# The weights' preparation and the first eight tiles of an FFN, in one order written out pass by pass

## The chip, the cores and the metric

The kernel runs on one core of a Trainium2 chip. The metric is the time of one execution on the device in microseconds (us). The engines go by the profile's names: PE is TensorE, DVE VectorE, ACT ScalarE, POOL GpSimd; SP issues most DMAs.

## The reference

The input x is 2 x 2048 x 256 in fp32. A feed-forward half step, an attention and a second half step are added to it, each after a layer norm without weights:

```python
x = x + 0.5 * ffn(layernorm(x), w_gate, w_up, w_down)
x = x + attn(layernorm(x), Wq, bq, Wk, bk, Wv, bv, Wo, bo)
x = x + 0.5 * ffn(layernorm(x), w_gate, w_up, w_down)

def fp4_quant_dequant(x):          # blocks of 16 along the last dimension
    scale = max(abs(xb)) / 6, at least 1e-12
    return (nearest of 0, .5, 1, 1.5, 2, 3, 4, 6 to abs(xb / scale)) * sign * scale
def fp4_linear(x, w): return fp4_quant_dequant(x) @ fp4_quant_dequant(w).T
def ffn(x): return fp4_linear(silu(fp4_linear(x, w_gate)) * fp4_linear(x, w_up), w_down)
```

w_gate and w_up are 704 x 256, w_down is 256 x 704. The attention has one head of complex numbers: scores from the real and imaginary parts of 512 projected columns, a softmax over 2048 positions, and an output projection. Both half steps use the same three weights.

## The kernel before

The 4096 tokens are 32 tiles of 128 tokens, kept in SBUF as four groups of eight (xs[0] to xs[3]). A tile lies with its tokens on the 128 partitions and 256 columns. All arithmetic is fp32.

**Rounding** (quant). One call rounds y to the fp4 grid, in place, for several tiles at once: a maximum over blocks (DVE), the scale and its reciprocal (DVE, small), a multiplication by the reciprocal (DVE, or POOL for weights), abs(y) x 2^22 into m (ACT), two DVE passes that add and subtract a multiple of the step so that y is rounded, and a multiplication by the scale ("last": mostly POOL). It is used on the weights (1536 columns of gate and of up, 1408 of down), on the normed inputs xl of four tiles (1024 columns), and on the hidden values h of two tiles (1408 columns).

**Weights.** gate_or_up(0), gate_or_up(1) and down() round a weight and transpose it on PE in blocks of 128 x 128 into wgu and wd, with ACT copying PSUM to SBUF. fold() multiplies the attention's weights with each other (wa, wvo and three vectors): 12 transposes and then matmuls on PE, copies on ACT.

**A half step** (ffn, a generator; `stage` is the one under way). For four tiles at a time, inputs(i0) computes the layer norm (statistics on DVE, a square root on ACT, the rest on DVE, the normed values on ACT), rounds them and transposes them into xqT. products(i) makes gate and up of tile i on PE, each in one of two PSUM buffers (p_big), then silu(gate) on ACT and the product with up on DVE, which goes to h. After two tiles, h is rounded. turn(i) transposes a tile's h on PE (ACT copies it to hqT) and back(i) multiplies it by wd on PE; DVE adds half of the result to x. Tile i's turn and back come two to four tiles after its products.

**Order.** The source emits whole steps one after another: fold(), then the first inputs(0), gate_or_up(0), gate_or_up(1), the first products, down(), and so on; `next(stage)` between them advances the half step by one tile. From this, the Tile framework's scheduler makes an order for each engine: it takes ready instructions by priority (their place in the source), so that passes of several steps mix on an engine, and puts in the semaphores between engines. An engine then works through its own list in order. In the loads, gate and up come first on SP's queue, then wq, wk, wv, wo, down, the second half of the first x group, and at last the other three groups.

```python
    fold()
    stage = ffn(0, False, ffn0_pools)
    next(stage)
    gate_or_up(0)
    gate_or_up(1)
    next(stage)
    down()
    next(stage)
    prep.close()
```

The attention and the second half step follow in later code, overlapped with the end of the first half step; the change leaves them as they are.

Of the kernel before, what the change touches and what calls it, by code (L numbers as in the profile page):

```python
# [10 lines left out]
FP = mybir.dt.float32  # L11
# [16 lines left out]
BELOW = 1.0 - 2.0**-22  # L28


@with_exitstack
def kernel(ctx: ExitStack, tc: tile.TileContext, x, wqT, bq, wkT, bk, wvT, bv, woT, bo,
# [44 lines left out]
    for name, w in (("gate", w_gate), ("up", w_up)):  # L77
        t = wpool.tile([P, NR, D], FP, tag=f"n_{name}", name=f"n_{name}")
        nc.gpsimd.memset(t[LAST:P, NR - 1, :], 0.0)
        nc.sync.dma_start(  # L80
            out=t[:, 0:NR - 1, :], in_=w[0:(NR - 1) * P, :].rearrange("(r p) k -> p r k", p=P)
        )
        nc.sync.dma_start(out=t[0:LAST, NR - 1, :], in_=w[(NR - 1) * P:FF, :])
        w_nat.append(t)
# [4 lines left out]
    for t, w in ((wq_sb, wqT), (wk_sb, wkT), (wv_sb, wvT), (wo_sb, woT)):  # L89
        nc.sync.dma_start(out=t, in_=w.rearrange("(k p) e -> p k e", p=P))  # L90
    wd_nat = wpool.tile([P, KD, FF], FP, tag="n_down", name="n_down")
    nc.sync.dma_start(out=wd_nat, in_=w_down.rearrange("(r p) k -> p r k", p=P))
    nc.sync.dma_start(out=xs[0][:, 4:GT, :], in_=x_g[0][:, 4:GT, :])
# [19 lines left out]
    wd = const.tile([P, NR, D], FP, tag="wd", name="wd")  # L113
    wa = const.tile([P, KD, D], FP, tag="wa", name="wa")
# [39 lines left out]
    def normalise(pool, g, j0, n):  # L154


        mv = pool.tile([P, n, 2], FP, tag="mv", name=f"mv{g}_{j0}")
        for j in range(n):
            st = pool.tile([P, 6], FP, tag="bn", name=f"bn{g}_{j0 + j}")
            nc.vector.bn_stats(st, xs[g][:, j0 + j, :])  # L160
            nc.vector.bn_aggr(mv[:, j, :], st)
        var = pool.tile([P, n], FP, tag="var", name=f"var{g}_{j0}")
        nc.vector.tensor_scalar(var, mv[:, :, 1], EPS, None, ALU.add)
        sd = pool.tile([P, n], FP, tag="sd", name=f"sd{g}_{j0}")
        nc.scalar.activation(sd, var, AF.Sqrt)
        rstd = pool.tile([P, n], FP, tag="rstd", name=f"rstd{g}_{j0}")
        nc.vector.reciprocal(rstd, sd)

        nc.vector.tensor_tensor(sd, rstd, rstd, ALU.mult)
        nc.vector.tensor_tensor(sd, sd, var, ALU.mult)  # L170
        nc.vector.tensor_scalar(sd, sd, -0.5, 1.5, ALU.mult, ALU.add)
        nc.vector.tensor_tensor(rstd, rstd, sd, ALU.mult)
        shift = pool.tile([P, n], FP, tag="shift", name=f"shift{g}_{j0}")
        nc.vector.scalar_tensor_tensor(shift, mv[:, :, 0], -1.0, rstd, ALU.mult, ALU.mult)
        return j0, rstd, shift

    def normed(dst, g, j, stats):
        j0, rstd, shift = stats
        k = slice(j - j0, j - j0 + 1)
        nc.scalar.activation(dst, xs[g][:, j, :], AF.Identity, bias=shift[:, k], scale=rstd[:, k])  # L180


    n_bank = 0

    def bank(shape, name):
        nonlocal n_bank
        n_bank += 1
        pool, tag = ((p_t, "t"), (p_acc, "acc"))[n_bank % 2]
        return pool.tile(shape, FP, tag=tag, name=name)
# [6 lines left out]
    def gate_or_up(which):  # L196

        t = w_nat[which]
        all_of(quant(wpool, t.rearrange("p r k -> p (r k)"), NR * D, "qw", nc.gpsimd, nc.gpsimd))
        for kc in range(KD):  # L200
            for r0 in range(0, NR, 4):
                rs = range(r0, min(r0 + 4, NR))
                ps = bank([P, 4, P], f"wt{which}_{kc}_{r0}")
                for r in rs:
                    nc.tensor.transpose(ps[:, r - r0, :], t[:, r, ts(kc, P)], ident)
                n = min(FF - r0 * P, 4 * P)
                nc.scalar.copy(
                    wgu[:, kc, ds(which * FF + r0 * P, n)], ps.rearrange("p r k -> p (r k)")[:, 0:n]
                )

    def down():
        all_of(quant(wpool, wd_nat.rearrange("p r k -> p (r k)"), KD * FF, "qw", nc.gpsimd, nc.gpsimd))
        nc.gpsimd.memset(wd[0:P - LAST, NR - 1, :], 0.0)
        for ic in range(NR):
            ps = bank([P, KD, P], f"wtd{ic}")
            for r in range(KD):
                nc.tensor.transpose(ps[:, r, :], wd_nat[:, r, chunk(ic)], ident)
            p0 = 0 if ic < NR - 1 else P - LAST
            nc.scalar.copy(wd[p0:P, ic, :], ps.rearrange("p r k -> p (r k)")[p0:P, :])

    def fold():
# [4 lines left out]
        for name, t in (("q", wq_sb), ("k", wk_sb), ("v", wv_sb)):  # L226
            e_sb = wpool.tile([P, KE, D], FP, tag=f"e_{name}", name=f"e_{name}")
            for c0 in range(0, KE, 2):
                ps = bank([P, 4, P], f"we_{name}{c0}")
                for c in range(2):  # L230
                    for kc in range(KD):
                        nc.tensor.transpose(ps[:, c * KD + kc, :], t[:, kc, ts(c0 + c, P)], ident)
                nc.scalar.copy(
                    e_sb[:, c0:c0 + 2, :].rearrange("p c d -> p (c d)"), ps.rearrange("p r k -> p (r k)")
                )
            nat[name] = e_sb
        for dst, left, right in ((wa, nat["q"], nat["k"]), (wvo, nat["v"], wo_sb)):
            for kc in range(KD):
                ps = bank([P, D], f"wm{kc}")
                for c in range(KE):  # L240
                    nc.tensor.matmul(
                        out=ps, lhsT=left[:, c, ts(kc, P)], rhs=right[:, c, :], start=(c == 0), stop=(c == KE - 1)
                    )
                nc.scalar.copy(dst[:, kc, :], ps)
        for kc in range(KD):
            ps = bank([P, 1], f"wb{kc}")
            for c in range(KE):
                nc.tensor.matmul(
                    out=ps, lhsT=nat["k"][:, c, ts(kc, P)], rhs=bq_sb[:, c:c + 1], start=(c == 0), stop=(c == KE - 1)
                )  # L250
            nc.scalar.copy(wkbq[:, kc:kc + 1], ps)
        for dst, row, right in ((wqbk, bk_sb, nat["q"]), (bout, bv_sb, wo_sb)):
            ps = bank([P, D], "wr")
            for c in range(KE):
                nc.tensor.matmul(
                    out=ps,
                    lhsT=row[:, c:c + 1].to_broadcast([P, P]),
                    rhs=right[:, c, :],
                    start=(c == 0),
                    stop=(c == KE - 1),  # L260
                )
            nc.scalar.copy(dst, ps)
        nc.gpsimd.tensor_tensor(bout, bout, bo_sb, ALU.add)
        bb = wpool.tile([P, KE], FP, tag="bb", name="bb")
        nc.gpsimd.tensor_tensor(bb, bq_sb, bk_sb, ALU.mult)
        ps = bank([P, KE], "wbb")
        nc.tensor.matmul(out=ps, lhsT=ones, rhs=bb, start=True, stop=True)
        nc.vector.tensor_reduce(bqbk, ps, AX.X, ALU.add)


    def ffn(phase, store, pools):
# [4 lines left out]

        def inputs(i0):

            g, j0 = divmod(i0, GT)
            if i0 < GT:  # L280
                stats[g] = normalise(small, g, j0, XT)
            elif j0 == 0:
                stats[g] = normalise(small, g, 0, GT)
# [5 lines left out]
            yield from quant(xp, xl.rearrange("p u d -> p (u d)"), XT * D, "qx", nc.gpsimd if i0 else nc.vector)  # L289
            yield  # L290
            xqT = xp.tile([P, XT, KD, P], FP, tag="xqT", name=f"xqT{phase}_{i0}", bufs=2)
            for u in range(0, XT, 2):
                ps = p_t.tile([P, 4, P], FP, tag="t", name=f"tx{phase}_{i0}_{u}")
                for v in range(2):
                    for kc in range(KD):
                        nc.tensor.transpose(ps[:, v * KD + kc, :], xl[:, u + v, ts(kc, P)], ident)  # L296
                nc.scalar.copy(
                    xqT[:, u:u + 2, :, :].rearrange("p u k t -> p (u k t)"), ps.rearrange("p r t -> p (r t)")
                )
            xqTs[i0] = xqT  # L300

        def products(i, xqT, h):
            halves = []
            for which in range(2):
                ps = p_big.tile([P, 2, 512], FP, tag="big", name=f"gu{phase}_{i}_{which}")
                for b2 in range(2):
                    for kc in range(KD):
                        nc.tensor.matmul(  # L308
                            out=ps[:, b2, 0:HALF],
                            lhsT=xqT[:, kc, :],  # L310
                            rhs=wgu[:, kc, ts(which * 2 + b2, HALF)],
                            start=(kc == 0),
                            stop=(kc == KD - 1),
                        )
# [478 lines left out]
```

## Time and profile before

| | |
|---|---|
| time, median of 3 runs | 1086.97 us (1086.94 to 1086.97) |
| the profiled execution: its own time, its span | 1089.07 us, 1087.3 us |
| mean granted clock of TensorE | 0.991 |
| first matmul, first gu matmul | 12.5 us, 44.2 us |
| DMA share, GB/s from 20 to 25 us; from 30 us on | 1.01, 419; near 0 |

The page gives busy times over the span, and then the span in 40 slices of 27.2 us with a digit for the share in tenths. A line of a group reads: source line, engine, operation, output and inputs, shapes and count, then busy time and mean nanoseconds of one, then the engine's idle time ahead of it and what ended that. Tiles are named as in the source: gu is the PSUM of gate and up (L308), po that of back (L335), th that of turn (L327), tx that of the inputs' transposes (L296); n_gate, n_up and n_down are the weights in their natural layout. A matmul of the source in fp32 stands in the profile as two instructions, a transpose as one. Passes of a DVE pass's line: L132 maximum, L138 or L143 (POOL) first multiplication, L147 abs on ACT, L148 and L150 the rounding, L152 last multiplication. The timeline gives start, duration, engine, line and operation of each instruction; an instruction's duration there includes the time that it is held up after it began.

### The profile page before, as it was taken

The page shows a single profiled execution, that of the slowest core. Times are in us where ns is not written, and L with a number is a line of the kernel's source. Part 1 is how long each engine was busy: PE and PEld are TensorE (multiplying, and loading weights), DVE is VectorE, ACT ScalarE, POOL GpSimd, SP SyncE. Part 2 cuts the span into 40 slices and gives each one's busy share as a digit, 9 for nine tenths or more (in the row PEclk, how much of TensorE's full clock was granted, in tenths as well). Part 3 has the DMA queues.
Part 4 walks back from the last instruction along what each step waited for, and adds up shares of the span by engine and source line. Part 5 has one row for each costly group of instructions (what it writes and reads, how often), then busy time and mean ns, then how long its engine had stood idle before and what let it go on. Part 6 is the DMA issues. An engine that isn't in the chain of part 4 may idle for free.

```text
span 1087.3 us, 11292 instructions
## 1 busy us (share of the span) xinstructions
PE 1050.2 (97%) x4206; PEld 737.0 (68%) x4206; DVE 816.3 (75%) x1359; ACT 472.1 (43%) x734; POOL 236.0 (22%) x135
## 2 busy tenths in 40 slices
PE   4698999999999999999999999999999999999998
PEld 4566777777776566667666666766655677777776
DVE  5999988886663798566588977768776597777575
ACT  3455545454335564346444453344343253433222
POOL 2413121211002111111113211212372112122110
PEclk9889999999999999999999999999999999999999
DMA  9000000000000000000000000000000000000001
GB/s 316 1 1 1 1 0 1 1 1 1 1 1 1 0 1 1 1 0 1 0 1 1 1 0 1 1 1 1 0 1 1 10 11 19 20 10 20 20 10 39
DMA packets 7270, 13.50 MB, mean 12 GB/s; under 512 B 1328, under 2 KB 3632, under 8 KB 6832
## 3 DMA queue, kind: packets, MB, share of 16 engines
q1 hardware_dynamic: 6112, 12.13, 3.1%
q10 hardware_dynamic: 1104, 0.66, 0.3%
q8 instruction: 33, 0.54, 0.2%
q14 instruction: 21, 0.17, 0.1%
HBM read 8.59 MB, written 4.19 MB: 12 GB/s over the span
## 4 chain that ended last, share of the span: by engine, by line
PE 87%; DVE 9%; ACT 2%; DMA 1%; issue 1%; POOL 1%; DVEq 0%; ACTq 0%; POOLq 0%
PE gu L308 26%; PE ps L494 18%; PE po L335 15%; PE m L591 14%; PE th L327 4%; PE poa L642 3%; PE z L569 2%; PE pu L472 2%; PE tx L296 1%; DVE st L529 1%; PE txa L410 1%; ACT xn L180 1%; DVE bn L160 1%; DMA x<-in_x_dram 0%; DMA n_up<-in_w_up_dram 0%
## 5 line engine op out<-in xcount | busy, mean ns | idle before, releaser
L308 PE MATMUL gu<-wgu,xqT 128*128 128x352 f32 x1024 | 320.6, 463 | 2.8 <-ACT h L318 2.8
L308 PEld LDWEIGHTS gu<-wgu,xqT 128*128 128x128 f32 x1024 | 190.1, 192 | 97.0 <-issue 4.4
L494 PE MATMUL ps<-uT,xT 128*128 128x512 f32 x512 | 232.3, 593 | 0.9 <-DVE most L506 0.9
L335 PE MATMUL po<-wd,hqT 128*128 128x256 f32 x768 | 176.3, 379 | 0.0
L335 PEld LDWEIGHTS po<-wd,hqT 128*128 128x128 f32 x768 | 144.9, 190 | 28.8 <-ACT zT L605 0.6
L494 PEld LDWEIGHTS ps<-uT,xT 128*128 128x128 f32 x512 | 95.1, 190 | 93.7 <-issue 81.2
L152 POOL TENSOR_TENSOR h<-h,qh_s 128x1408 f32<-128x1408 f32 x30 | 78.7, 2622 | 326.1 <-DVE h L150 250.5
L506 DVE TENSOR_TENSOR most<-ps,most 128x512 f32<-128x512 f32 x112 | 77.0, 687 | 92.9 <-ACT st L501 92.3
L501 ACT COPY st<-ps 128x512 f32<-128x512 f32 x128 | 74.5, 583 | 127.9 <-PE ps L494 127.5
L328 ACT COPY hqT<-th 128x512 f32<-128x512 f32 (+1 forms) x128 | 55.4, 481 | 170.6 <-PE th L327 168.5
L591 PE MATMUL m<-tw,xn 128*128 128x256 f32 x448 | 124.6, 379 | 0.0
L558 POOL TENSOR_TENSOR sums<-tw,sums 128x512 f32<-128x512 f32 x42 | 57.9, 1378 | 230.1 <-DVE tw L554 198.9
L530 ACT ACTIVATE st<-st 128x1024 f32<-128x1024 f32 x64 | 67.4, 1057 | 77.3 <-DVE st L529 76.8
L591 PE MATMUL m<-st,xn 128*128 128x256 f32 x336 | 100.0, 379 | 0.0
L319 DVE TENSOR_TENSOR h<-h,gu 128x704 f32<-128x704 f32 x64 | 56.4, 882 | 56.8 <-PE gu L308 54.3
L591 PEld LDWEIGHTS m<-tw,xn 128*128 128x128 f32 x448 | 85.0, 190 | 12.5 <-DVE tw L550 0.6
L529 DVE TENSOR_TENSOR st<-st,top 128x1024 f32<-128x1024 f32 x64 | 83.2, 1311 | 0.8 <-ACT top L525 0.8
L591 PEld LDWEIGHTS m<-st,xn 128*128 128x128 f32 x336 | 63.2, 190 | 26.2 <-issue 19.1
L148 DVE SCALAR_TENSOR_TENSOR h<-qh_m,h 128x1408 f32<-128x1408 f32 (+1 forms) x34 | 53.5, 1574 | 34.3 <-ACT qh_m L147 34.1
L318 ACT ACTIVATE h<-gu 128x704 f32<-128x704 f32 x64 | 48.2, 753 | 50.9 <-PE gu L308 50.9
L147 ACT ACTIVATE qh_m<-h 128x1408 f32<-128x1408 f32 (+1 forms) x34 | 44.4, 1306 | 44.2 <-DVE h L138 40.7
L327 PE MATMUL th<-ident,h 128*128 128x128 f32 x384 | 52.8, 273 | 1.1 <-ACT hqT L328 1.1
(156 smaller groups left out, 1239.8 us busy)
## 6 DMA issues: line engine op xcount, KB each, us to landing
out_dram<-x SPq DMA_DIRECT2D x15, 256.0 KB, 2.1
x<-in_x_dram SPq DMA_DIRECT2D x3, 1024.0 KB, 13.1
n_down<-in_w_down_dram SPq DMA_DIRECT2D x1, 704.0 KB, 8.2
n_gate<-in_w_gate_dram SPq DMA_DIRECT2D x1, 640.0 KB, 6.8
n_up<-in_w_up_dram SPq DMA_DIRECT2D x1, 640.0 KB, 8.3
x<-in_x_dram ACTq DMA_DIRECT2D x1, 512.0 KB, 5.3
wq_sb<-in_wqT_dram SPq DMA_DIRECT2D x1, 512.0 KB, 4.8
wk_sb<-in_wkT_dram SPq DMA_DIRECT2D x1, 512.0 KB, 5.6
```

What stands on the lines that cost most here:

```text
L152: last.tensor_tensor(yb, yb, scale.unsqueeze(2).to_broadcast([P, nb, BLK]), ALU.mult)
L308: nc.tensor.matmul(out=ps[:, b2, 0:HALF], lhsT=xqT[:, kc, :], rhs=wgu[:, kc, ts(which * 2 + b2, HALF)], start=(kc == 0), stop=(kc == KD - 1),)
L319: nc.vector.tensor_tensor(h, h, up, ALU.mult)
L327: nc.tensor.transpose(ps[:, r - r0, :], hq[:, chunk(r)], ident)
L335: nc.tensor.matmul(out=po, lhsT=hqT[:, r, :], rhs=wd[:, r, :], start=(r == 0), stop=(r == NR - 1))
L494: scored = nc.tensor.matmul(out=ps, lhsT=gr.of.xT[s][:, c, v, :], rhs=gr.uT[:, c, :], start=(c == 0), stop=(c == KD - 1),)
L501: nc.scalar.copy(piece[:, v, :], ps)
L506: seen = nc.vector.tensor_tensor(gr.most, ps, gr.most, ALU.max)
L529: nc.vector.tensor_tensor(piece, piece, gr.top.unsqueeze(1).to_broadcast([P, 2, Q]), ALU.subtract)
L530: nc.scalar.activation(piece, piece, AF.Exp, scale=SCALE)
L558: add(gr.sums, t[:, 1:3, :], gr.first[:, 1:3, :] if s == 1 else gr.sums, ALU.add)
L591: i = nc.tensor.matmul(out=gr.m[k], lhsT=left, rhs=right, start=first, stop=last)
```

## The change

The weights' preparation and the first eight tiles become 36 generators ("threads"), each of which yields after a single pass: f (fold), g0, g1, u0, u1 (halves of gate and of up, 768 columns each), d0, d1 (halves of down, 704 columns), n0, n1, n2 (layer norm statistics of tiles 0-3, 4-7, 8-15), x0 to x5 (inputs of two tiles each, 512 columns, tiles 0 to 11), p0 to p7 (products of a tile), h0 to h3 (rounding of two tiles' h), t0 to t3 and b0 to b3 (turn and back of a tile). A string in the source, ORDER, names 264 steps; each takes the named thread's next pass. Each instruction of the opening gets a dependency without a semaphore on the one ahead of it in its engine's list (fence), so the scheduler keeps that order; close_fences() does the same between the opening's last instruction on each engine and everything emitted later.

Beside that:
- ON_POOL says for each thread whether the first and the last multiplication are on POOL. For h0 to h3 the first goes from DVE to POOL; for x0 and x1 both are on DVE, as they were for the first four tiles.
- A small step of the reciprocal on the POOL way is a tensor_scalar instead of a scalar_tensor_tensor with ones.
- The loads: gate in two parts with wq between and wk behind, then up, wv, wo, the second half of the first x group, down. One load more.
- The memset of wd is emitted at the start. The last sum of fold is an accumulation on ACT, not a reduction on DVE. The weights' PSUM tiles come from p_acc alone, not from p_t and p_acc in turn. h has four buffers in the first half step, not three.
- After the opening, the half step goes on from tile 8 with tiles 4 to 7 waiting for their turn.

```diff
+ORDER = """
+n0 n0 n0 g0 g0 g0 g0 n0 n0 g0 n0 g1 n0 g1 n0 f n0 g1 g0 n0 f g0 f n0 f g1 n0 g0 g1 x1 u1 x0 x1 u0 x0
+f g1 f u0 g0 u1 g1 f x0 x1 g1 u0 x0 f n1 u1 g1 f f n1 u0 x0 n1 x0 x1 f n1 n1 u1 x1 n1 d1 u0 u1 x1 u0
+n2 g1 n1 n2 n1 f u1 x0 d1 g1 n1 x0 x1 x0 n1 f u1 g0 x0 n1 x1 g0 p0 n1 x3 u1 u0 x2 p1 u1 n2 p0 d0 u1
+x3 x1 u0 u0 x3 d0 d1 n2 d0 d1 d1 u1 p1 n2 x2 n2 u0 n2 x3 u0 x2 d0 x3 x1 n2 x3 x2 n2 p0 x3 x2 n2 d1
+x2 d0 n2 p0 d0 n2 x3 n2 p1 p3 x2 p1 n2 x2 f n2 d0 h0 p3 d1 d0 h0 n2 p2 d1 p2 h0 x3 x4 x3 p3 x4 h0 x4
+p3 p2 x2 p2 x4 x5 x5 h1 d0 x2 x5 p6 p4 x4 h0 h0 p6 p5 h1 x4 h0 p4 d1 x4 h0 x4 h1 p5 p4 p5 h1 h0 h1
+x5 p4 d0 p5 p7 x4 h1 h2 d1 t0 p7 d1 x5 h1 x5 h2 t0 h1 p6 x5 p6 h2 h2 t1 p7 h1 h2 p7 h3 x4 d0 t1 x5
+h2 b0 h3 t2 h3 x5 h3 t2 h2 b1 b0 t3 x5 h2 t3 h3 b1 h3 h3 b2 h2 h3 b3 b2 b3 h3
+"""
+TURNED = 4
...
+    load_rows(w_nat[0], w_gate, 0, NH)
+    nc.sync.dma_start(out=wq_sb, in_=wqT.rearrange("(k p) e -> p k e", p=P))
+    load_rows(w_nat[0], w_gate, NH, NR)
+    nc.sync.dma_start(out=wk_sb, in_=wkT.rearrange("(k p) e -> p k e", p=P))
+    load_rows(w_nat[1], w_up, 0, NR)
+    nc.sync.dma_start(out=wv_sb, in_=wvT.rearrange("(k p) e -> p k e", p=P))
+    nc.sync.dma_start(out=wo_sb, in_=woT.rearrange("(k p) e -> p k e", p=P))
+    nc.sync.dma_start(out=xs[0][:, 4:GT, :], in_=x_g[0][:, 4:GT, :])
     nc.sync.dma_start(out=wd_nat, in_=w_down.rearrange("(r p) k -> p r k", p=P))
-    nc.sync.dma_start(out=xs[0][:, 4:GT, :], in_=x_g[0][:, 4:GT, :])
...
+    class Rounding:
...
+        def turns(self, y, n):
...
+            nc.vector.tensor_reduce(scale, yb, AX.X, ALU.max, apply_absolute_value=True)
+            yield
+            nc.vector.scalar_tensor_tensor(scale, scale, 1.0 / 6.0, tiny.to_broadcast([P, nb]), ALU.mult, ALU.max)
+            yield
+            rec = self.tile("r", nb, self.bufs)
+            nc.vector.reciprocal(rec, scale)
+            yield
+            if self.first:
+                nc.vector.tensor_scalar(rec, rec, BELOW, None, ALU.mult)
+                yield
+                nc.gpsimd.tensor_tensor(yb, yb, by_block(rec), ALU.mult)
+            else:
+                nc.vector.scalar_tensor_tensor(yb, yb, BELOW, by_block(rec), ALU.mult, ALU.mult)
+            yield
+            m = self.tile("m", n, self.bufs_m)
+            nc.scalar.activation(m, y, AF.Abs, scale=STEPS)
+            yield
+            nc.vector.scalar_tensor_tensor(y, m, LEAST, y, ALU.max, ALU.add)
+            yield
+            nc.vector.scalar_tensor_tensor(y, m, LEAST, y, ALU.max, ALU.subtract, reverse1=True)
+            yield
+            (nc.gpsimd if self.last else nc.vector).tensor_tensor(yb, yb, by_block(scale), ALU.mult)
+            yield
...
+        def products(i):
+            gate = product(0, i)
+            yield
+            h = hs[i].rearrange("p (c i) -> p c i", c=2)
             nc.scalar.activation(h, gate, AF.Silu)
+            yield
+            up = product(1, i)
+            yield
             nc.vector.tensor_tensor(h, h, up, ALU.mult)
+            yield
...
+        for name in ORDER.split():
+            next(threads[name])
...
+        fence(begun)
+        return 8, list(range(TURNED, 8)), norms["n2"]
...
-    fold()
     stage = ffn(0, False, ffn0_pools)
     next(stage)
-    gate_or_up(0)
-    gate_or_up(1)
-    next(stage)
-    down()
-    next(stage)
     prep.close()
...
+    close_fences()
```

## The prediction

> **What bounds the kernel now.** I read the page's slices first, then the windows, the groups of TensorE up to 150 us, the chain and the timeline. The page:
>
> ```profile
> PE 1050.2 (97%) x4206; PEld 737.0 (68%) x4206; DVE 816.3 (75%) x1359; ACT 472.1 (43%) x734; POOL 236.0 (22%) x135
> PE   4698999999999999999999999999999999999998
> DVE  5999988886663798566588977768776597777575
> POOL 2413121211002111111113211212372112122110
> PEclk9889999999999999999999999999999999999999
> ```
>
> TensorE is full from the fourth slice (82 us) on. Before that it is not, and there DVE is at 9. The windows (time, PE, PEld, DVE, ACT, POOL, clock, DMA, GB/s):
>
> ```profile
> 35.00:40.00 5.00, 1.08 (x5) 1.08 (x6) 5.00 (x7) 0.00 (x0) 2.12 (x1) 0.65 0.00 0
> 50.00:55.00 5.00, 1.48 (x5) 0.71 (x5) 5.00 (x9) 1.86 (x2) 2.59 (x1) 0.86 0.00 0
> 105.00:110.00 5.00, 2.88 (x13) 2.13 (x12) 5.00 (x7) 1.73 (x4) 1.93 (x1) 0.82 0.02 3
> ```
>
> DVE is never idle while TensorE starves, and the granted clock sags after each gap. How much TensorE loses I take from counts, since its busy time holds slow matmuls too. Dense prices are in the chain of waits:
>
> ```profile
> 114.83 2.59 PE po L335 x12
> 117.42 0.66 PE th L327 x6
> 118.08 4.74 PE gu L308 x16
> ```
>
> So 0.296 us for a gu matmul, 0.216 for one of 256 columns, 0.11 for a transpose of h or weights, 0.13 for one of x. The groups up to 150 us:
>
> ```profile
> L308 PE MATMUL gu<-wgu,xqT 128*128 128x352 f32 x208 | 67.7, 477 | 2.8 <-ACT h L318 2.8
> L335 PE MATMUL po<-wd,hqT 128*128 128x256 f32 x95 | 21.8, 379 | 0.0
> L296 PE MATMUL tx<-ident,xl 128*128 128x128 f32 x40 | 7.0, 332 | 8.0 <-DVE xl L152 4.5 <-POOL xl L152 3.5
> ```
>
> 208 x 0.296 + 95 x 0.216 + 40 x 0.13 + 48 transposes of h x 0.11 = 92.6, and fold() with the weights' transposes 19.1 at the same prices: 111.7 us of work in 150. **TensorE loses 38.3 us**, 34.6 of it by 86 us; from 150 us on it is dense, so what the change takes off the 38.3 comes off the end.
>
> Who holds DVE shows in the timeline:
>
> ```profile
> 28.90 1.22 DVE L148 SCALAR_TENSOR_TENSOR xl<-qx_m,xl 128x1024 f32<-128x1024 f32 x1
> 29.13 3.66 POOL L152 TENSOR_TENSOR n_gate<-n_gate,qw_s 128x1536 f32<-128x1536 f32 x1 [8.44 <-DVE n_gate L150]
> 30.04 4.37 DVE L148 SCALAR_TENSOR_TENSOR n_up<-qw_m,n_up 128x1536 f32<-128x1536 f32 x1
> 74.63 2.60 POOL L152 TENSOR_TENSOR h<-h,qh_s 128x1408 f32<-128x1408 f32 x1 [10.51 <-DVE h L150]
> 75.74 1.56 DVE L132 TENSOR_REDUCE qh_s<-h 128x88 f32<-128x1408 f32 x1
> ```
>
> The POOL pass that began under a DVE pass took 3.66 instead of 2.80, and the DVE pass issued next 4.37 instead of 1.75: it ended one pass length after POOL did. A POOL multiplication and a DVE pass with two SBUF inputs run one after the other; a maximum (75.74) runs beside POOL undisturbed. Of the nine large POOL passes up to 86 us (22.6 us at their own length), 7.4 us, a third, has DVE work of the undisturbed kind beside it: nearly all of the passes at 37.88 and 74.63, little of the rest.
>
> The Trainium skill (SBUF — State Buffer, "Who interferes with whom") says the same of this port pair, an exclusive lock, and so speaks against a part of this change: giving POOL the first multiplication of h frees DVE of no port time. The trace agrees (4.37); the sum below goes by the rows alone.
>
> **The change, part by part.** The opening (weights and eight tiles) keeps its arithmetic; its passes become smaller and their order is written out per engine, with everything later behind it. Prices for the new sizes n by lines through rows: a DVE pass 0.07 + 0.00104 n (1.14, 1.53, 1.67 us at 1024, 1408, 1536 in the chain of waits), a POOL pass 0.22 + 0.00168 n (1.93, 2.59, 2.80). A half of gate or up (768) costs 0.87 on DVE and 1.51 on POOL; a pair of x tiles (512) 0.60 and 1.08; half of down (704) 0.80 and 1.40; a pair of h 1.53 and 2.59; a small one 0.10 on DVE. Halving thus adds about 0.07 to 0.2 us a pass; it is in the sums.
>
> *DVE's queue up to the point that matters.* TensorE has two PSUM buffers for products, so gate of tile 6 ("p6") waits until DVE has multiplied tile 3 ("p3", fourth step). Ahead of that, counted in ORDER: 12 half-weight passes 10.4; 19 x passes 11.4; 6 of down 4.8; one maximum of h 1.5; three h*up at 0.87, 2.6; 16 bn_stats at 0.34, 5.4, with aggregates 1.9; reciprocals 4.0; 34 small ones 3.4. Sum 45.5. It begins when x lands, 6.1 (DVE's first row).
>
> *POOL meanwhile:* 8 x 1.51 + 3 x 1.40 + 2 x 1.08 + 0.85 for fold's sums = 19.3. Laying DVE's maxima, bn_stats, reciprocals and h*up (PSUM input: 0.88 us at 74.48 under POOL as elsewhere) beside these passes in the order given, all are covered but x2's last (1.1), d0's last (0.9), g0's last (1.0), u0's last (0.7) and scraps: 5.0 us of stall.
>
> *Waits of DVE for loads and ScalarE:* before, 0.3 + 1.15 + 4.07 and small ones, near 6, the 4.07 being for the normed x behind copies on ScalarE. The order puts a second thread wherever ScalarE is in the chain; between 0 and 6 I take 3.
>
> So p6 starts at 6.1 + 45.5 + 5.0 + 3 = 59.6. TensorE has then done fold 15.5, half-weights 2.6, four x transposes 2.1, eight half products 19.0: 39.2. **Lost 20.4.** The first product starts near 30 (44.2 before), the first "up" near 39.
>
> *After p6:* 34.3 us of TensorE work (eight half products 19.0, down 1.3, x 1.1, turns and backs of four tiles 2.6 + 10.4), dense to 94, then tile 8's products to 98.7, then the turn of tile 4, which needs h2's last POOL pass. DVE up to h3's add, which runs ahead of that pass: 45.5 + 27.2 (seven x passes 4.2, ten h passes 15.3, five h*up 4.4, the rest 3.3) = 72.7. POOL ahead of it 38.4, of which 10.5 uncovered (h3's first 2.2, h2's first 1.1, h0's last 0.9 are the new ones of size). 6.1 + 72.7 + 10.5 + 2.6 + 3 = 94.9, before 98.7: no new stall.
>
> *Moved work.* h's first multiplication to POOL: 4 x 1.53 off DVE, 4 x 2.59 on POOL, both inside these sums; alone it is worth between -6.1 and +4.2. fold(), scattered over TensorE's gaps, costs nothing while those gaps exist (15.5 of work before p6, 20.4 lost); were they gone it would cost its length, as now. Its last reduction goes from DVE (0.15) to ScalarE, which was busy 37.9 of the 80 us from 6 to 86. The memset of wd goes to POOL's start: 0.3 hidden in its wait for the first maximum. Loads: wq second in SP's queue instead of fifth lands ahead of 12.5, where TensorE now begins; up lands some 2.5 us later (two 0.5 MB loads ahead at 400 GB/s, the windows' rate at 15 us), near 13.8, as DVE reaches it; x's second half goes ahead of down, both used past 19. One more load costs SP 0.5 us of issuing, ahead of all later loads, hidden likewise.
>
> *The pins.* Whatever waits holds all behind it on its engine: ScalarE's first copy of fold waits for wq with the absolute value of the first gate half behind it, and DVE's add behind that; this is in the 3 us. The end of the opening pins tile 8 and the inputs of tile 12 behind it; those are needed only at some 127, and DVE has 32 us for some 27 of work (one x of 1024, two h, four h*up, norms at the prices above).
>
> Remaining loss: 20.4, 1 for a sagging clock where TensorE waits for "up", 1 for stalls past p6 (3.7 past 86 before). 22.4 against 38.3 leaves a gain of 15.9.
>
> On the clock: the Trainium skill (TensorE: Matmul & The Clock Gate, Part 1) has half rate after an idle window of about 3.4 us until one busy window is over. The trace agrees in kind (0.65 in 35 to 40); by that rule a gap costs up to 1.7 us, and the sum with two more would be 3.4 us worse.
>
> The profiled execution took 1089.07 with a span of 1087.3; the median is 1086.97. The sum is made on the span's loss and its difference carried to the median: **1071 us**.
>
> **Rivals.** All turn on how much of POOL's time is covered, and on the waits.
> - *Covered as little as now, a third.* Ahead of h2's last pass: 6.1 + 72.7 + 25.7 + 2.6 + 3 = 110.1 against 78.3 of TensorE work: 31.8 lost, with 2 as above 33.8, a gain of 4.5: 1082.5. For it: no engine's order is tied to another's, so a shift of 1 us puts a POOL pass over another DVE pass than intended. Against: long runs of maxima and statistics stand where POOL runs.
> - *Slower: POOL locks DVE throughout.* The end rises with each uncovered us. With nothing covered, 38.4 in place of 25.7: 44.5 + 2 lost, 8 us slower: 1095. It decides where cover falls under 22%. For it: at 15.10 and 44.15 tiny DVE steps took 2.77 and 2.29 us under POOL, the new order has 24 large POOL passes up to h3 where the old one has 12, and a pinned DVE cannot go round a locked step. Against: the third reached now.
> - *Better.* Cover of 85% and 1 us of waits: 6.1 + 45.5 + 2.9 + 1 - 39.2 = 16.3, with 0.5 more 16.8, a gain of 21.5: 1065.5.
>
> **Numbers.** A measurement here can tell 0.2% (2.2 us) from no change. Forecast, 1066.5 to 1077: 0.55. Little cover, 1077 to 1084.8: 0.22. Better: 0.10. Slower: 0.10. Between, within 0.2%: 0.03. The likeliest is 1071; the range 1064 to 1084 leaves out about 0.05 below and 0.14 above. Faster 0.87, same 0.03, slower 0.10.
>
> **What would show it.** Right: first gu matmul near 30 and not 44, a dense TensorE from about 60, h2's last POOL pass ending near 95, the 150 us mark reached with some 16 us more TensorE work done, no change of the rest. Wrong: DVE passes of two inputs at 2.5 to 4 us in a row, h2's last pass past 105, TensorE gaps behind the opening, or another time in the rest of the kernel, whose order the scheduler chooses.

## The result, and the profile after

After: 1074.16 us, the median of 4 runs (1073.74 to 1074.85); before, beside it, 1086.97 (1086.94 to 1087.64, 4 runs). The ratio is 0.9881, 95% interval 0.9864 to 0.9898: 12.8 us faster, 3.2 us above the forecast of 1071. The profiled execution of after took 1073.74, with a span of 1071.9 and a mean granted clock of 1.000.

The page, busy times and the first lines of the slices (now 26.8 us each):

```profile
PE 1044.7 (97%) x4206; PEld 731.6 (68%) x4206; DVE 805.8 (75%) x1387; ACT 469.9 (44%) x739; POOL 253.6 (24%) x148
PE   6998999999999999999999999999999999999998
DVE  7999998867634888576688958678767587777575
POOL 4563121210103020111124111212461021221110
```

TensorE is at 9 from the second slice on, but for the fourth and the last, which are at 8 as they were before. POOL is busier in the first slices, and DVE has 10.5 us less of busy time over the span. The windows (time, PE, PEld, DVE, ACT, POOL, clock, DMA, GB/s), the three of before and one where a gap now lies:

```profile
35.00:40.00 5.00, 4.72 (x26) 3.29 (x26) 5.00 (x23) 3.74 (x9) 4.30 (x3) 1.00 0.00 0
50.00:55.00 5.00, 5.00 (x21) 3.34 (x20) 4.60 (x10) 3.25 (x7) 4.86 (x3) 1.00 0.00 0
95.00:100.00 5.00, 2.96 (x11) 1.57 (x9) 5.00 (x8) 1.70 (x2) 0.00 (x0) 1.00 0.01 2
105.00:110.00 5.00, 5.00 (x26) 3.96 (x25) 4.27 (x13) 4.49 (x7) 0.00 (x0) 1.00 0.00 0
```

In 50 to 55 all engines work at once. In 95 to 100 TensorE stands while DVE is full, as it did before in the opening. The groups of TensorE up to 150 us:

```profile
L428 PE MATMUL gu<-wgu,xqT 128*128 128x352 f32 x240 | 74.6, 461 | 2.4 <-DVE h L446 2.0 <-ACT xqT L404 0.3
L472 PE MATMUL po<-wd,hqT 128*128 128x256 f32 x120 | 27.5, 380 | 0.0
L403 PE MATMUL tx<-ident,xl 128*128 128x128 f32 x40 | 5.8, 275 | 3.9 <-POOL xl L184 3.9
...
L330 PE MATMUL we_q<-ident,wq_sb 128*128 128x128 f32 x8 | 1.9, 420 | 8.1 <-DMA wq_sb<-in_wqT_dram 8.1
```

240 gu matmuls stand where 208 did, and 120 of po where 95 did. At the prediction's dense prices 128.5 us of work are done by 150: TensorE loses 21.5 where it lost 38.3. The loss over time, so counted, in us:

| up to | 50 | 70 | 88 | 110 | 150 | 250 |
|---|---|---|---|---|---|---|
| before | 26.5 | 33.5 | 34.4 | 37.5 | 38.3 | 38.1 |
| after | 15.0 | 14.7 | 15.1 | 19.5 | 21.5 | 22.4 |

The last column counts the attention's first transposes too (txa, 0.13 each). So the opening gained 19.3 by 88, and 3.6 of it are given back between 88 and 250; the 15.7 that are left are near the 15.3 by which the two profiled executions differ. TensorE in the timeline:

```profile
30.88 5.00 PE L428 MATMUL gu<-wgu,xqT 128*128 128x352 f32 x16 [0.35 <-ACT xqT L404]
38.08 7.60 PE L428 MATMUL gu<-wgu,xqT 128*128 128x352 f32 x24
...
97.73 2.63 PE L428 MATMUL gu<-wgu,xqT 128*128 128x352 f32 x8 [2.04 <-DVE h L446]
102.41 1.09 PE L403 MATMUL tx<-ident,xl 128*128 128x128 f32 x8 [2.04 <-POOL xl L184]
125.81 1.09 PE L403 MATMUL tx<-ident,xl 128*128 128x128 f32 x8 [1.85 <-POOL xl L184]
```

From 31 to 88 us TensorE loses 1 us in all; the gaps at 97.7, 102.4 and 125.8 are the ones behind the opening. The locks between DVE and POOL:

```profile
21.34 0.68 DVE L277 SCALAR_TENSOR_TENSOR xl<-xl,qx_r 128x512 f32<-128x512 f32 x1
21.50 1.87 POOL L275 TENSOR_TENSOR n_up<-n_up,qw_r 128x768 f32<-128x768 f32 x1
62.48 1.86 DVE L273 TENSOR_SCALAR qh_r<-qh_r 128x88 f32<-128x88 f32 x1
79.96 3.90 POOL L275 TENSOR_TENSOR h<-h,qh_r 128x1408 f32<-128x1408 f32 x1
81.67 3.67 DVE L285 SCALAR_TENSOR_TENSOR h<-qh_m,h 128x1408 f32<-128x1408 f32 x1
```

L275 is the first multiplication on POOL, L277 the one on DVE, L273 the small step ahead of it, L285 the second rounding pass. At 21.50 POOL began second and paid (1.87, 1.49 alone); at 62.48 and 81.67 DVE paid: 1.86 (the pass of POOL there lasts from 61.38 to 64.28), where the same step took 0.19 with no POOL pass beside it at 80.22 in the kernel without closing pins below; and 3.67 in place of 1.62, behind POOL's pass of 79.96. That pass had itself paid before (3.90 in place of 2.59), as DVE's pass of 79.81 was under way. I took each pass's time above the usual one of its shape (excesses over 0.05 us) up to 88.1: DVE was held 7.5 us and POOL 6.2, with 47.9 us of POOL's passes. Before it was 10.5 and 1.7, with 26.4.

### The profile page after: what moved, and what is told of

It is laid out like the page before. It is cut to its first block, busy times and chain, and to the rows that moved or that the text cites. A ratio compares the mean times of both kernels' runs of the same rounds, so it can differ in the third digit from the quotient of the medians.

```text
span 1071.9 us, 11329 instructions
## 1 busy us (share of the span) xinstructions
PE 1044.7 (97%) x4206; PEld 731.6 (68%) x4206; DVE 805.8 (75%) x1387; ACT 469.9 (44%) x739; POOL 253.6 (24%) x148
## 4 chain that ended last, share of the span: by engine, by line
PE 89%; DVE 7%; ACT 2%; DMA 1%; issue 1%; POOL 0%; SPq 0%; DVEq 0%; ACTq 0%; POOLq 0%
PE gu L428 26%; PE ps L708 19%; PE m L805 15%; PE po L472 14%; PE th L463 4%; PE poa L856 3%; PE pu L686 2%; PE z L783 2%; PE tx L403 1%; DVE st L743 1%; PE wm L338 1%; PE txa L624 1%; ACT xn L234 1%; DVE h L285 1%; DVE h L283 1%
## 5 line engine op out<-in xcount | busy, mean ns | idle before, releaser
L184 POOL TENSOR_TENSOR h<-h,qh_s 128x1408 f32<-128x1408 f32 x26 | 67.5, 2595 | 294.0 <-DVE h L182 252.1
L180 DVE SCALAR_TENSOR_TENSOR h<-qh_m,h 128x1408 f32<-128x1408 f32 (+1 forms) x30 | 45.8, 1527 | 33.1 <-ACT qh_m L179 32.9
L442 ACT ACTIVATE h<-gu 128x704 f32<-128x704 f32 x64 | 48.2, 753 | 44.9 <-PE gu L428 44.6
L179 ACT ACTIVATE qh_m<-h 128x1408 f32<-128x1408 f32 (+1 forms) x30 | 38.9, 1297 | 45.9 <-DVE h L170 42.1
```

Source lines behind the costliest of these rows:

```text
L184: last.tensor_tensor(yb, yb, scale.unsqueeze(2).to_broadcast([P, nb, BLK]), ALU.mult)
```

## The experiments

Times are medians, and the loss is TensorE's, counted as above. The main theory: the gain is the order, pinned on each engine, by which POOL's passes lie beside DVE passes that they don't hold. The rivals: the parts alone make it (smaller passes, the loads, h's multiplication on POOL), or DVE's sum of work decides and not the locks.

The kernel before was timed anew with each group of runs, with medians from 1086.96 to 1087.85. For the three changes of 2.2 to 3.0 us below, the interval of the ratio overlaps with that of after; that they are slower rests on their times, all of which are above the slowest of after (1074.85), and on the loss counted by 150 us (24.3 to 25.6, after 21.5).

**Without the pins.** The same passes, emitted in the same order; the scheduler sets each engine's list.

```diff
-        fence(begun)
...
-    close_fences()
```

> The changed kernel without its fences: the same single passes emitted in the same order, but the scheduler is free to reorder on each engine. Theory A (the gain is the order itself, DVE and POOL passes laid beside each other): the scheduler departs from it, DVE is locked more often by POOL; 1077 to 1085, over 3 us slower than the changed kernel's 1074.2. Theory B (the gain comes from smaller passes and from emitting the threads together; the pins do nothing): 1073 to 1076.

1085.76 (1083.52 to 1086.48, 11 runs; the profiled one, 1083.62, is among the fastest); ratio to before 0.9978 (0.9969 to 0.9987). Of the 12.8 us all but 1.4 need the pins: smaller passes, loads and POOL's multiplications without them are worth next to nothing. The loss by 88 us is 25.4 (after 15.1). Locks are only a part of these 10.3: DVE was held 11.1 us, 3.6 more than in after, with less work of POOL (39.2 us). Other parts stand in TensorE's waits, of which ScalarE's list has two:

```profile
PE we_k L330 <- ACT e_q L331: 3.7, 1, 3.7
PE po L472 <- ACT wd L313: 3.3, 1, 3.3
```

The columns are the sum, the number and the longest, up to 150 us. The first was 1.4 in after; the second, from 85.4 to 88.6, isn't there in after. The first gu comes at 34.55. How the 10.3 divide between locks and the rest isn't shown. So the theory holds for the order as a whole and is too narrow in naming the locks alone.

**Pinned, but thread after thread.** The other bound of the same theory: the 264 steps in the order f, n0, x0, x1, g0, g1, u0, u1 and so on, each thread to its end.

> The changed kernel with its 264 steps in another order, as pinned: each thread runs to its end before the next begins (fold, n0, x0, x1, g0, g1, u0, u1, n1, x2, x3, p0, p1, h0 and so on). Theory A (the gain is the weave; pins without it keep every engine waiting for the one step under way): the opening's DVE 75 us, POOL's 43 and ScalarE's share of the chains add up with little beside each other, TensorE loses 60 to 90 us in place of 15: 1105 to 1145. Rival (fixed lists of smaller passes do it in any sensible order): 1074 to 1087.

1202.4 (ratio 1.1051, 1.1036 to 1.1067), slower than even the theory gave. One window (columns as above), and the longest of TensorE's waits up to 150 us:

```profile
50.00:75.00 25.00, 4.63 (x18) 3.42 (x18) 15.59 (x24) 6.13 (x10) 10.43 (x8) 0.50 0.00 0
PE wtd L311 <- POOL n_down L287: 25.4, 2, 20.5
```

No engine is full: each waits for another in turn. The loss is 110.2 us by 150, and 143.8 by 250: tile 8 onwards has been held behind it all. Of the 110.2, TensorE stands still for 95.7, so the waits alone exceed the theory's 60 to 90. Another 14.9 are matmuls slower than the dense prices; the theory's price had left out the clock, 0.50 in this window. Pins alone don't gain; the weave that they hold does.

**Without the closing pins only.** Order pinned inside the opening; later work may be placed among it.

```diff
-    close_fences()
```

> The orders stay pinned inside the opening, but the work written behind it is free to be placed among it by the scheduler (the closing fences are left out). Theory: the pinned order of the opening is what gains, and the closing fences only keep later work behind it, so 1072 to 1078 with the first gu product still near 31 us and TensorE's loss up to 50 us near 15 us. Rival: work of tiles 8 to 12 placed among the opening takes VectorE's and POOL's time from the chain to h, loss up to 88 us of 18 us or more, 1078 to 1086.

1076.71 (ratio 0.99, 0.9883 to 0.9916): 2.5 slower than after. First gu at 30.53 and loss by 50 us of 15.6, as the theory had it, but by 88 us 20.8, as its rival had it:

```profile
78.09 2.20 DVE L180 SCALAR_TENSOR_TENSOR xl<-qx_m,xl 128x1024 f32<-128x1024 f32 x1
81.13 3.03 DVE L182 SCALAR_TENSOR_TENSOR xl<-qx_m,xl 128x1024 f32<-128x1024 f32 x1
...
88.03 1.11 PE L403 MATMUL tx<-ident,xl 128*128 128x128 f32 x4 [2.37 <-POOL xl L287]
```

L180 and L182 round tile 12's inputs, work due over 20 us later, and they are held (2.20 and 3.03, some 1.2 alone); the last multiplication of the opening's own inputs then comes 8 us later on POOL (86.92, after 78.77), and TensorE waits for it. Part of the loss comes back by 150, since those inputs are done: 24.7 against 21.5.

**h's first multiplication back on DVE.** The weave is the same, without the four small steps.

```diff
-    ... "h0": (True, True), "h1": (True, True), "h2": (True, True), "h3": (True, True),
+    ... "h0": (False, True), "h1": (False, True), "h2": (False, True), "h3": (False, True),
```

> The changed kernel with the first multiplication of h0 to h3 back on DVE (four steps fewer in the order). By the port (a POOL pass and a two-input DVE pass run one after the other) 4 x 2.59 us of POOL go and 4 x 1.53 us of DVE come: between 4 us faster and 1 us slower, as the opening's end or only its cover counts: 1070 to 1075. By DVE's busy time alone, which is what the step in the change would be for: 3 to 6 us slower, 1077 to 1080.

1080.55 (ratio 0.9932, 0.9919 to 0.9944): 6.4 slower than after, a miss of the port theory, and 0.5 beyond what DVE's busy time alone gave. DVE was held 4.8 us by 88, 2.7 less than in after, but it has 6.1 us more of its own work, and what remains is still locked:

```profile
65.36 3.28 DVE L277 SCALAR_TENSOR_TENSOR h<-h,qh_r 128x1408 f32<-128x1408 f32 x1
67.13 2.43 POOL L287 TENSOR_TENSOR xl<-xl,qx_s 128x512 f32<-128x512 f32 x1
```

The loss is 19.0 by 88 and 30.1 by 150. So the four POOL passes, 10.4 us long, cost DVE 2.7 us and freed it of 6.1; the rest lay mostly beside maxima, reciprocals and h*up.

**h's first multiplication of tiles 8 to 15 on POOL too**, where no order is written out.

```diff
-            all_of(quant(later["pool"], h, n * FF, "qh", nc.gpsimd if n == HT else nc.vector))
+            ahead = nc.gpsimd if first and i0 < 16 else None
+            all_of(quant(later["pool"], h, n * FF, "qh", nc.gpsimd if n == HT else nc.vector, ahead))
```

> The changed kernel, where the four pairs of tiles behind the opening (tiles 8 to 15) too have h's first multiplication on POOL. Theory A (TensorE's 6.4 us lost between 88 and 150 us are DVE's backlog; taking four passes of 1.54 us off DVE takes most of it away, as the same four passes cost 6.4 us in the opening): 3 to 5 us faster, 1069 to 1071. Rival (there POOL's 4 x 2.59 us lock DVE out of its two-input passes): 0 to 4 us slower, 1074 to 1078.

1080.54 (ratio 0.9931, 0.9919 to 0.9944): 6.4 slower than after, the way of the rival and beyond its 0 to 4. The move that gains 6.4 in the weave loses 6.4 outside it. One reason stands at 108.07, 0.2 us behind the start of a POOL pass (107.89 to 110.48):

```profile
108.07 2.43 DVE L221 TENSOR_TENSOR rstd<-rstd,sd 128x8 f32<-128x8 f32 x1
```

A step on 8 numbers a partition, 0.15 us alone, waits for that pass to end; another, at 153.05, takes 2.35. The move isn't quite the same, either: the small step ahead of the multiplication is a scalar_tensor_tensor with two SBUF inputs here, which took 1.71 at 128.67 and 1.56 at 151.15 under POOL's passes (0.23 elsewhere). Loss up to 250 us: 29.3, after 22.4.

**The small step ahead of POOL's multiplication moved to POOL**, at its old place in the order.

```diff
-                nc.vector.tensor_scalar(rec, rec, BELOW, None, ALU.mult)
+                nc.gpsimd.tensor_scalar(rec, rec, BELOW, None, ALU.mult)
```

> The changed kernel with the small step in front of POOL's first multiplications (a tensor_scalar on 44 to 88 columns) on POOL in place of DVE. On DVE, this step took 1.86 and 1.07 us at 62.5 and 74.3 where POOL was in a pass, and 0.2 us elsewhere. Theory A (a tensor_scalar in SBUF is locked out by POOL as a two-input pass is): the step leaves DVE's queue, some 3 us of DVE time go, POOL gains ten small steps of 0.2 to 0.3 us in its idle time: 1 to 3 us faster, 1071 to 1073. Rival (the step merely shows a wait that the next DVE pass would take in its place): no change, 1073.5 to 1075.

1079.84 (ratio 0.9927, 0.9914 to 0.9941): 5.7 slower, a miss. The step was put into POOL's list where DVE's had stood:

```profile
53.00 0.43 POOL L273 TENSOR_SCALAR qh_r<-qh_r 128x88 f32<-128x88 f32 x1 [6.37 <-DVE qh_r L270]
53.40 1.06 POOL L287 TENSOR_TENSOR xl<-xl,qx_s 128x512 f32<-128x512 f32 x1
```

POOL stood 6.37 us for DVE's reciprocal, with the last multiplication of x2 behind it: 53.40, after 45.97. A pinned list turns one misplaced step of 0.4 us into a stall of everything behind it.

**The same, with the step directly ahead of its multiplication in the order.**

> The small step on POOL once more, but with its place in the order moved right in front of the multiplication that it serves, so that it holds nothing else in POOL's list. The earlier run, 1079.8, had it ahead of x2's last multiplication, which started at 53.4 in place of 46.0, behind the small step's wait for a reciprocal of h0. Theory A (that place alone made it slower, and the tensor_scalar on DVE was locked out by POOL for some 3 us): 1 to 3 us faster than the changed kernel, 1071 to 1073. Rival (POOL's small step is itself on the path, 0.3 to 0.4 us in each of ten chains, or DVE's gain moves to another wait): 1073.5 to 1077.

1076.32 (ratio 0.9893, 0.988 to 0.9907): the wait is gone, and it is still 2.2 slower. DVE was held only 4.4 us by 88, but the step lengthens each chain to h: 0.32 to 0.98 us on POOL, up to 1.80 when DVE holds it, for 0.2 to 0.36 on DVE where POOL did not hold it for long. That this is the reason isn't shown: by 88 us only 0.9 more is lost than in after (16.0), and the rest comes behind the opening (24.3 by 150).

**The loads in the old order** (gate and up, then wq, wk, wv, wo, down, x's second half).

> The changed kernel with the loads in the order of the kernel before (gate, up, wq, wk, wv, wo, down, x's second half). Theory A (a pinned list waits for its slowest item): ScalarE's copy of fold's first transposes waits for wq near 12.5 in place of 8.1, and behind it stands the absolute value of gate's first half, 11.3 in the changed kernel; DVE's first add goes from 12.4 to some 15.5, and 2 to 4 us reach the end: 1076 to 1078. Rival (DVE has other work to put there and TensorE's start doesn't count): 1073.5 to 1075.

1077.15 (ratio 0.9898, 0.9883 to 0.9913): 3.0 slower. The first transposes begin 4.5 us later (12.66, after 8.11), and, through the copy on ScalarE that is pinned ahead of the absolute value of gate, DVE's first rounding pass at 15.15 (12.35). Loss by 50 us: 17.9, after 15.0.

**Behind the opening: tile 12's inputs emitted two tiles later.**

```diff
-            if i0 % XT == 0 and i0 + XT < NT and i0 + XT not in xqTs:
+            if i0 % XT == 0 and i0 + XT < NT and i0 + XT not in xqTs and i0 != first:
                 all_of(inputs(i0 + XT))
+            if first and i0 == first + HT:
+                all_of(inputs(first + XT))
```

> The changed kernel with the inputs of tile 12 emitted two tiles later, behind the products of tiles 8 and 9 in place of ahead of them. In the changed kernel TensorE stands still for 2.0 us before 97.7 and 2.0 us before 102.4, where DVE does these inputs before it multiplies h of tile 8. Theory A (the stalls come from that place in the source alone): both gaps vanish and nothing takes their place, 4 us faster, 1069.5 to 1071. Rival (DVE is behind by then whatever it does first, so the wait only moves to tile 12 or 16): 1073 to 1076.

1073.96 (ratio 0.9874, 0.986 to 0.9887), no change, as the rival said. The wait at 102.4 went, and one of 3.84 for the same kind of input came at 128. DVE's list hardly changed up to 101 us: tile 8's h*up, now earlier in the source, still began at 96.80 behind tile 12's first passes (96.81 in after). That isn't because it wasn't ready: pinned ahead, in the last run below, it began at 93.77.

**Only the transposes later.** Inputs stay where they are but for the transposes and their copies, which are emitted ahead of the products of the group's last tile. The edit reaches all five groups behind the opening, not only the two that the expectation names.

```diff
-            if i0 % XT == 0 and i0 + XT < NT and i0 + XT not in xqTs:
-                all_of(inputs(i0 + XT))
+            to = i0 - i0 % XT + XT
+            if first and (i0 % XT == 0) and to < NT:
+                coming = inputs(to)
+                for _ in range(7):
+                    next(coming)
+            elif not first and i0 % XT == 0 and to < NT and to not in xqTs:
+                all_of(inputs(to))
...
             for u in range(n):
+                if first and to < NT and i0 + u == to - 1:
+                    all_of(coming)
                 all_of(products(i0 + u))
```

> In the two groups of four tiles behind the opening (tiles 8 to 11 and 12 to 15), only the transposes of the next group's inputs and their copies are written later, just ahead of the products of the group's last tile; the additions, multiplications and quantization of those inputs stay where they are. Theory: after the opening TensorE stands for work that its own written order puts ahead of work that is ready: in the changed kernel it waits 2.6 us at 99.8 to 102.4 and 2.8 us at 123 to 125.8 for an input tile to be transposed, while products of tiles already prepared lie behind. Then both waits vanish, the one at 95.7 to 97.7 (2.0 us, for tile 8's h) stays, and the time falls by 3 to 5 us to 1069 to 1071. Rival: VectorE's work behind the opening sets the pace, and the waits come back at the next product; then 1073 to 1075, with TensorE's loss up to 150 us still 21 to 22 us.

1069.41 (ratio 0.9832, 0.9817 to 0.9846), 4.8 faster than after, as the theory gave. The first gaps left behind the opening, in the timeline of TensorE:

```profile
98.61 2.63 PE L428 MATMUL gu<-wgu,xqT 128*128 128x352 f32 x8 [1.39 <-DVE h L446]
113.53 1.06 PE L403 MATMUL tx<-ident,xl 128*128 128x128 f32 x8 [0.46 <-ACT hqT L464]
```

The transposes wait for no input any more. Between 88 and 150 us TensorE loses 2.3 where after lost 6.4. DVE's passes are the same, up to 101 us in the same order and then in another: TensorE had stood behind its own list.

**Both of these together.**

> As the kernel with the late transposes, and tile 12's whole inputs are written two tiles later as well, so that VectorE multiplies tiles 8 and 9 first. Theory of the written order: all three waits of TensorE behind the opening (2.0, 2.6 and 2.8 us of the changed kernel, at 97.7, 102.4 and 125.8) vanish, loss up to 150 us near 15 to 16 us, time 1067 to 1070. Rival, VectorE's sum of work behind the opening: the wait is only moved to 120 to 135 us, 1072 to 1075.

1069.3 (ratio 0.9831, 0.9816 to 0.9846): nothing on top. In that stretch DVE's list came out as in the kernel with late transposes, tile 8's h*up behind tile 12's inputs again, so the gap of 1.39 stayed.

**Late transposes, and tile 8's h*up pinned ahead** of all later DVE work but one maximum.

```diff
-                for _ in range(7):
+                for _ in range(3 if i0 == first else 7):
                     next(coming)
...
+                if first and i0 + u == first:
+                    multiplied = nc.cur_bb.bb.instructions[-1]
+                    fences.append((multiplied, {multiplied.engine: multiplied}))
+                    for _ in range(4):
+                        next(coming)
```

> The kernel with the late transposes, and beside it all of VectorE's work written behind the opening, but for the maximum of tile 12's inputs, is pinned behind tile 8's multiplication h*up. In the kernel with late transposes that multiplication began at 97.70 us, behind statistics and tile 12's inputs, and TensorE stood 1.4 us for it ahead of 98.61. Theory: VectorE's order alone makes this wait. Then h*up begins near 95, TensorE has no gap there, the loss up to 150 us is 16.5 to 17.5 us instead of 18.5, and the time is 1067.5 to 1069. Rival: VectorE's sum of work sets the pace and the 1.4 us come back at a later product or transpose before 150 us; 1069 to 1070.5.

1072.58 (ratio 0.986, 0.9844 to 0.9877): slower by 3.2 than without the pin, though the pin did what it should. h*up began at 93.77, and TensorE loses nothing from 88 to 130. But the list behind the pin came out otherwise. Three small steps of a layer norm stand under passes of POOL (the first of these passes is shown with them):

```profile
111.72 2.59 POOL L184 TENSOR_TENSOR h<-h,qh_s 128x1408 f32<-128x1408 f32 x1 [7.96 <-DVE h L182]
111.83 2.50 DVE L215 TENSOR_TENSOR sd<-rstd 128x8 f32<-128x8 f32 x1
133.74 2.22 DVE L215 TENSOR_TENSOR sd<-rstd 128x8 f32<-128x8 f32 x1
136.22 1.63 DVE L217 TENSOR_TENSOR sd<-sd,var 128x8 f32<-128x8 f32 x1
...
139.58 2.63 PE L428 MATMUL gu<-wgu,xqT 128*128 128x352 f32 x8 [1.91 <-DVE h L446]
```

They take 6.35 us where 0.45 would do, 5.9 too much; without the pin there are two such steps (2.10 at 116.71 and 1.43 at 135.71), 3.2 too much. TensorE then stands 1.91 at 139.6 and 2.26 at 148.5, and its loss goes from 15.5 by 130 us to 20.3 by 150. The second wait ends on ScalarE's copy of hqT, which stood behind four norms of the attention (145.78 to 147.84), so the small steps aren't the whole cause. That a later wait would come was the rival; its size was in neither.

The fastest version run is the change with late transposes, 1069.4, with the two together level with it.

## Why the prediction was right, and where its steps were not

**The mechanism held.** The first product at 30.88 (near 30), the first "up" at 38.08 (near 39), TensorE dense through the opening, two-input DVE passes and POOL's multiplications one after the other, maxima beside them. That the written order carries the gain is shown by the same passes without pins: 1.4 us in place of 12.8. That it does so by the cover of POOL alone is not: there DVE was held 3.6 us more, of 10.3 us lost.

**The opening was over-priced by 5.3 us of loss (20.4, measured 15.1).** The queue to "p3 h*up" ends 6.5 us earlier, 5.6 of it in the stalls and waits:

| | forecast | measured |
|---|---|---|
| DVE's work | 45.5 | 44.6 |
| held by POOL | 5.0 | 2.0 |
| waits for loads and ScalarE | 3 | 0.4 |
| ends at | 59.6 | 53.08 |

Measured: busy 46.56 us in the window from 6.11 to 53.08, of which 2.0 are above the usual times, and the rest idle. I had laid each uncovered POOL pass on DVE. But it is the second to begin that waits, and on this stretch POOL was held 4.2 us and DVE 2.0; POOL had idle time to spare. Measured so, cover is 82% up to h2's last pass (7.5 of the 41.7 us that POOL's passes take undisturbed); the sum had 10.5 uncovered of 38.4, 73%. The "better" rival had 85%. Before, the holding counted in this way is 10.5 of 24.7 us, 43%, where the prediction's count left two thirds uncovered. Two of its readings were a little off as well: the first small step under POOL began at 15.18 (POOL's pass at 15.10), and POOL's pass of 37.88, counted as nearly all covered, had itself been held (3.67 instead of 2.80).

**So p6 is no longer the point that decides.** Its gate, the ninth half product, begins at 53.72, behind other products and with no wait. Of the 15.1 us lost by 88, 14.0 are lost by 31: 8.1 wait for wq, 1.4 the copy behind its transposes, and most of the rest slow first matmuls (16 of them in the 4.65 us behind 13.58, where dense ones take 3.5). The forecast's 20.4 rested on a queue that had become shorter than TensorE's own work. h2's last POOL pass ended at 88.08 (94.9).

**"No new stall" was wrong, by 5.4 us.** 1 us was put down for stalls past p6; 6.4 are lost between 88 and 150. The argument was a sum, 32 us of DVE time for some 27 of work. The sum was nearly enough, but sums hide lists: TensorE stood at 102.4 and 125.8 for transposes that its own list had ahead of ready products. The kernel with late transposes shows it: the same DVE work, 4.1 us less lost there. The rest of the kernel stays nearly as it was: 0.9 are lost from 150 to 250, most of it in one wait of 0.65 at 170.32, where before lost nothing.

**The total came out by two errors of opposite sign:** 22.4 lost forecast, 21.5 measured at 150 us. That these agree so well is luck: the opening lost 5.3 less than forecast and the stretch behind it 5.4 more.

**The step to the median failed by 2.5 us.** Before's executions lie mostly at two levels, near 1087 and near 1089 (in one group of nine runs also between), and the profiled one (1089.07, clock 0.991) is of the upper. Between the profiled executions the gain is 15.3, as against 15.9 forecast; between the medians it is 12.8. So some 2 us of the profiled execution were not in the median; that they belong to the 38.3 that I counted is likely, as TensorE is dense behind, but no execution of the lower level was profiled. Then the difference should have come off the loss, not been carried over.

**"Alone worth between -6.1 and +4.2"** for h's first multiplication: 6.4 us in the time, beyond the good end. The Trainium skill (SBUF — State Buffer, "Who interferes with whom") speaks of an exclusive lock, for which the issue order decides who is blocked. The trace agrees with both (1.87 on POOL at 21.50, 3.67 on DVE at 81.67). What I drew from it, that POOL frees DVE of no port time, the run with h on DVE refutes: four passes cost 2.7 us of holding for 6.1 of work.

**The clock.** The prediction's sentence on two more gaps, 3.4 us, did not come about: gaps of 2.0 us behind the opening leave 1.00 in 95 to 100. That agrees with the idle window of about 3.4 us that the Trainium skill gives (TensorE: Matmul & The Clock Gate, Part 1), and so does the 0.50 of the thread-after-thread kernel, where TensorE works 4.63 us of 25. A gap longer than that stands in the kernel with tile 12's inputs later: behind the wait of 3.84 us the clock is 0.58 from 127.9 to 132.0. One row stays unexplained: after 8.1 us without a matmul at the start, the clock reads 1.00 from 5 to 10 and 10 to 15, though the first matmuls are slow.

**The slower rival** needed cover below 22%; measured by holding, DVE paid for 18% of POOL's time in after and for 31% (11.1 of 35.9) without the pins, so cover was 82% and 69%.

## What to carry to other kernels

Where two engines share a lock, price an order and not an average: write out which pass lies beside which, pin it, and ask of each pair which begins second and whether that engine has time to spare. A pinned or scheduled list is a queue, so look at the first wait behind the stage that you improved: moving the transposes of one engine's list, with no work saved, was worth 4.8 us, over a third of what the whole change gained. And compare the profiled execution with the median before carrying a loss counted in it over to the time.

## What was not expected of the hardware

- Very small DVE steps can pay the whole rest of a POOL pass. A tensor_tensor on 8 numbers a partition took 2.50, 2.22, 1.63 and 2.43 us (0.15 alone); the first began 0.11 us behind POOL's pass of 111.72 and ended with it (114.33 and 114.31). A tensor_scalar with one SBUF input was held as well: all four on 88 numbers (L273, 0.23 to 1.86 us) began under a POOL pass and ended 0.06 us behind it, among them the one at 62.48 under the pass of 61.38 to 64.28; one on 4 numbers took 0.96 (L206 at 9.73).
- The holding is about as large on POOL's side (6.2 us by 88) as on DVE's (7.5). POOL has idle time there, and none of TensorE's waits up to 88 us ends on POOL.
